# Summing a block's last two bunches in one step, and moving the stores and the reads of its rows, in a two-layer graph network kernel

## The chip, the cores and the metric

One core of a Trainium2 chip runs the whole kernel. The time is the device time of one execution in microseconds (us). Three runs of the kernel before the change took 3989.87, 3995.48 and 4023.41 us; the median is 3995.48.

Five engines take part: PE (matrix products; PEld is its loading of weights), DVE (vector operations), ACT (functions and copies), POOL (here it only issues the gathers) and SP (here it only issues transfers). Each has its own queue of instructions, carries them out in order, and waits for the others by semaphores.

## What is computed

A graph has 12500 nodes with 128 features and 200000 edges, sorted by their destination. An edge's relation is one of ten, the argmax of ten of its 42 attributes. A layer takes the mean of the source rows over the edges of each (destination, relation), multiplies it by that relation's matrix, sums over the relations, and adds the node's own row times a root matrix and a bias:

```python
def _rgcn_layer(x, src, dst, edge_type, w_rel, root, bias):
    seg = dst * NUM_REL + edge_type
    xs = x[src]
    sums = segment_sum(xs, seg, N * NUM_REL)
    cnt = segment_sum(ones, seg, N * NUM_REL)
    mean = (sums / maximum(cnt, 1.0)[:, None]).reshape(N, NUM_REL, -1)
    return einsum('nrd,rdo->no', mean, w_rel) + x @ root + bias
h = relu(_rgcn_layer(x, ..., w_rel1, root1, b1))
out = layernorm(x + _rgcn_layer(h, ..., w_rel2, root2, b2))
```

## The kernel before, in words

**Tiles and bunches.** The edges lie in 1563 tiles of 128 (`NT`), in the order of their destination. Four tiles make a bunch (`QB`, line 31), so layer 1 has 391 bunches and walks them in steps `p` (loop at line 948). A tile's work is this. POOL gathers the 128 source rows from DRAM by an indirect transfer into a tile `g` (`gathered`, line 751). DVE builds a mask `oh` that holds, for each edge, a one in the column of its relation and its destination within a window of twelve nodes (`ones`, line 765), and ACT scales it by one over the count (`weighted`, line 757). PE multiplies the gathered rows by the mask into a PSUM tile `zp` (line 983). DVE adds that into `cc`, a ring in SBUF that holds the sums of 1024 nodes for ten relations (`sum_into`, line 797). The window's place in the ring is a register that DVE loads.

**Two layers at once.** The ring has two halves, one for each layer. A node's hidden row `h` is final when all edges into it have been added; since edges are sorted, nodes become final in order, in blocks (`starts`: 46 of 256 nodes, then six of 128 or less). Once a block is final its hidden rows are stored into a table `XH`, beside the input rows. Later tiles gather from that table rows of 256 features, input and hidden, and PE multiplies both parts, so that an edge whose source is already known is done for both layers in one gather. An edge whose source isn't known yet finds zeros there. What was missed is done in layer 2: the first `T0` tiles, gathered before the table was of use, are gathered again from the full hidden table `hD`, and the missed edges of the later tiles are regrouped on the chip into new tiles and gathered from `hD` too (lines 1461 to 1537).

**Two tables and epochs.** There are two copies of `XH`, because a copy can't be written while gathers read it. Epochs are counted in rows of 11 tiles (`RT`). From epoch k on (`first_seen[k]`, line 125) gathers read the copy that holds the rows of all blocks up to k; the next epoch reads the other copy (`table_of`, line 127). A block's rows go into the copy of its own epoch first (`stored(hb, first, k)`, line 875), and into the other copy once that epoch has begun (line 879). Which tile first reads a block is fixed ahead by a rule: `finished_in(k)` (line 109) is the step that finishes block k, and the epoch begins `READY` bunches (six, line 54) behind that step, rounded up to a whole row of 11 tiles. The same rule fixes `T0` (166 tiles) and the size of what layer 2 regroups.

**The order of the work around a block's end.** The order on each engine is the order in which the program is written (a manual schedule, line 1042). A step p issues the gathers of bunch p, the products of bunch p on PE (`products`, line 976), then side jobs, then the sums of bunch p - 2 (`BEHIND`, line 37; `sums`, line 986). Where the bunch just summed is the last that a block needs, `finish(k, t)` (line 844) follows in the same step: PE projects the block by ten matrices and the root (`projected`, line 732, lines 739 and 742). The rest is put off to later steps by a list of due times, in units u of one bunch: `rows_out` after one step (ACT adds the bias and cuts off below zero, line 672; PE turns the rows, line 864), `rows_kept` after two (ACT copies them, line 871; SP stores them into `hD` and the table), the clearing of the ring's places (line 722), the second layer's projection (`second`) after three, the load and the turning of the next block's input rows.

**Buffers.** `g` has seven buffers (`GB`); once the table is read a bunch takes one of them, so the gather of bunch p needs the products of bunch p - 7 done. `zp` has five PSUM tiles, two a bunch. `oh` has seven. The turned and projected blocks (`pf`) share two PSUM tiles.

The lines that matter most:

```python
q = p - BEHIND                                            # 988
while done < NBLK and t0 + n >= done_after(done):         # 1002
    finish(done, t)
...
assert k <= K0 or now + QB >= first_seen[k - 1]           # 877
...
todo.at(t + (1 if k == NBLK - 2 else 2) * u, rows_kept)   # 892
```

Of the kernel before, what the change touches and what calls it, by code (L numbers as in the profile page):

```python
# [30 lines left out]
QB = 4  # L31
# [5 lines left out]
BEHIND = 2  # L37
# [13 lines left out]
SPLIT = 63  # L51
LEAD = 40
LAST = 40
READY = 6
LOW = 1 << 13
TOPN = (1 << 14) - 1
OFF = 80
# [7 lines left out]
def rgcn_resnorm_kernel(ctx: ExitStack, tc: tile.TileContext, x, src, dst, attr, w_rel1, root1, b1,  # L65
# [26 lines left out]
    def done_after(k):  # L92

        if k == NBLK - 1:
            return NT
        f = starts[k + 1] / N
        t = int((E * f + 5 * (E * f * (1 - f)) ** 0.5) / P) + 2
        if t >= NT:
            return NT
        return min(a + n for a, n in parts if a + n >= t)  # L100
# [7 lines left out]

    def finished_in(k):

        return -(-done_after(k) // QB) - 1 + BEHIND

    K0, K1 = KSEEN
    NR = (NT - QB * (finished_in(K0) + READY)) // RT
# [722 lines left out]
    def layer_1():  # L837

        todo = Later()
        done = 0  # L840
# [3 lines left out]
        def finish(k, t):  # L844

            if k < NBLK - 2:
                todo.run(END)
            if k not in fTs:
                xbs[k] = rows_in(k)
                fTs[k] = features_in(k, 0, xbs[k])  # L850
            u = QB if t < NT else 0
            folded(ALL, k, WN)
            po = [projected(k, 0, (rsb[0], fTs[k]))]
            both = starts[k + 1] > bounds(T0)[0] if k + 1 < NBLK else True
            reused = starts[k] + RN < N
            assert not reused or t + 7 * u <= (starts[k] + RN - OFF - WN) // STEP

            def rows_out(_):
                a = po.pop()
                a = fin_a.setdefault(k, shifted(a, k, 0))  # L860
                pr = ps_f.tile([P, 4, C], F32, name="pf")
                n0, n, subs = block(k)
                for i, h in subs:
                    nc.tensor.transpose(pr[:h, i, :], a[:, i * P:i * P + h], ident)
                po.append(pr)

            def rows_kept(now):
                pr = po.pop()
                hb = fin.tile([P, 2, C], F32, name=f"hb{k % 2}")
                for p, s in spans(k):  # L870
                    nc.scalar.activation(hb[:p, s], pr[:p, s], AF.Copy)
                rows_dma(hb, hD, k, True)
                if k <= K1:
                    first = 0 if k <= K0 else (k - K0) % 2
                    stored(hb, first, k)
                    if k < K1:
                        assert k <= K0 or now + QB >= first_seen[k - 1]
                        when = t + 8 * QB if k < K0 else first_seen[k] + 2 * QB
                        todo_late.append((when, lambda t: stored(hb, 1 - first, k)))

            def second(_):
                po.append(projected(k, 1, (rsb[1], fin_a.pop(k)), more=both))

            def second_kept(_):
                n0, n, _ = block(k)
                p2 = po.pop()
                t2 = fin.tile([P, 3 * P], F32, name="v")
                nc.scalar.activation(t2[:, :n], p2[:, :n], AF.Identity, bias=bsb[1])
                nc.sync.dma_start(T2[:, n0:n0 + n], t2[:, :n])

            todo.at(t + u, rows_out)
            todo.at(t + (1 if k == NBLK - 2 else 2) * u, rows_kept)
            if reused:
                todo.at(t + 2 * u, lambda t: cleared(0, k, 0))
                todo.at(t + 3 * u, lambda t: cleared(0, k, 1))
            if k < NBLK - 1:
                todo.at(t + (9 if k >= NBLK - 3 else 3) * u, second)
                todo.at(t + (9 if k >= NBLK - 3 else 4) * u, second_kept)
            else:
                todo.run(t)  # L900
                todo.run(END)
                todo.at(t, second)
                todo.at(t, second_kept)
            if both:
                w = 10 if k >= NBLK - 3 else 5
                todo.at(t + w * u, lambda t: cleared(1, k, 0))
                todo.at(t + (w + 1) * u, lambda t: cleared(1, k, 1))
            if k + 1 < NBLK - 1:
                def fetch(t):
                    xbs[k + 1] = rows_in(k + 1)  # L910

                def turn(t):
                    n0, n, subs = block(k + 1)
                    pt = ps_f.tile([P, YB], F32, name="pf")
                    for i, h in subs:
                        nc.tensor.transpose(pt[:, i * P:i * P + h], xbs[k + 1][:h, i, :], ident[:h, :h])
                    po.append(pt)

                def turned_kept(t):
                    n0, n, subs = block(k + 1)  # L920
                    pt = po.pop()
                    fTs[k + 1] = fin.tile([P, 3 * P], F32, name="fT")
                    nc.scalar.activation(fTs[k + 1][:, :n], pt[:, :n], AF.Copy)  # L923
                todo.at(t + u, fetch)
                w = 2 if k == NBLK - 3 else 4
                todo.at(t + w * u, turn)
                todo.at(t + (w + 1) * u, turned_kept)
# [20 lines left out]
        for p in range(-AHEAD, NPT + BEHIND):  # L948
            if p + AHEAD < NPT:
                t0, n = parts[p + AHEAD]  # L950
                ohs[p + AHEAD] = ones(keyE[:, t0:t0 + n], iotaP, n, WN)
            if 0 <= p + AHEAD - 1 < NPT:
                t0, n = parts[p + AHEAD - 1]
                for j in reversed(range(n)):
                    weighted(ohs[p + AHEAD - 1], j, KW, wE[:, t0 + j:t0 + j + 1])
            if p < 0:
                continue
            t = p * QB
            if p < NPT:
                t0, n = parts[p]  # L960
                plain = t0 + n <= T0
                if not plain or p % 2 == 0:
                    g = gpool.tile([P, GQ * C], F32, name="g")
                slot = [p % 2 * QB + j if plain else 2 * j for j in range(n)]
                for j in range(n):
                    i = t0 + j
                    idx = idxE[:, i:i + 1]
                    if i < T0:
                        gathered(g, slot[j], x, idx, 1)
                    else:  # L970
                        gathered(g, slot[j], XH[table_of(i)], idx, 2)
                made = (g, ohs.pop(p), slot)
            if p == NPT - CP // 4:
                xbs[NBLK - 1] = rows_in(NBLK - 1)
                fTs[NBLK - 1] = features_in(NBLK - 1, 0, xbs[NBLK - 1])
            def products(g, oh, slot):
                t0, n = parts[p]
                zps[p] = [ps_z.tile([P, YB], F32, name="zp") for _ in range(0, n, 2)]
                for j in range(n):
                    i = t0 + j  # L980
                    zp, a = zps[p][j // 2], j % 2 * 2 * KW
                    for l in (0, 1) if i >= T0 else (0,):
                        nc.tensor.matmul(zp[:, a + l * KW:a + (l + 1) * KW], g[:, (slot[j] + l) * C:(slot[j] + l + 1) * C],  # L983
                                         oh[:, j * KW:(j + 1) * KW], start=True, stop=True)

            def sums():
                nonlocal done, offs, row
                q = p - BEHIND
                if q < 0:
                    return  # L990
                t0, n = parts[q]
                if t0 % CT == 0:
                    row = rows_.tile([1, CT], I32, name="row")
                    nc.scalar.dma_start(row, b_i[t0 // CT:t0 // CT + 1, :])
                if t0 % G == 0:
                    m = min(G, NT - t0)
                    offs = offsets(row[:, t0 % CT:t0 % CT + m], t0, m, bounds)
                for j in range(n):
                    i = t0 + j
                    sum_into(ALL if i >= T0 else ONE, zps[q][j // 2], j % 2 * 2 * KW, offs[i % G], WN)  # L1000
                del zps[q]
                while done < NBLK and t0 + n >= done_after(done):
                    finish(done, t)
                    done += 1

            if p < NPT - 1:
                products(*made)
            jobs.run(t)
            sums()
            if p == NPT - 1:  # L1010
                products(*made)
            made = None
            todo.run(t)
            for d in [d for d in todo_late if d[0] <= t]:
                todo_late.remove(d)
                d[1](t)
# [692 lines left out]
```

## Time and profile before

| what | value |
|---|---|
| median of three runs | 3995.48 us (3989.87 to 4023.41) |
| the profiled execution | 4014.34 us |
| its span, first to last instruction | 4012.5 us |
| mean granted PE clock, share of full | 0.759 |
| gathers of x alone, of the table, of `hD` in layer 2 | 166; 1397; 166 + 695 |
| layer 1, by POOL's gathers | up to about 2557 us |
| bytes read from DRAM, written | 322.86 MB, 57.89 MB |

How to read it: the page gives for each engine its busy time, for groups of instructions their line, operation, tiles, count, busy time and mean, and then the idle time that the engine had before them and what ended it. "issue" is idle time that nothing in the profile ended, "remote" an end that the profile can't name. The view of waits adds up such idle times by engine and line: total us, times, longest. The timeline has one row for an instruction or a run of like ones: start, duration, engine, line, operation, count, and in brackets the idle time ahead of it with its releaser. The view of stretches has for each stretch of time the busy time and the count (x) of each engine, of all its instructions or of one line's.

### The profile page before, as it was taken

To read this page: it belongs to the slowest core of one execution; us is meant where nothing else is said; L and a number is where in the kernel's file an instruction comes from. 1 tells how busy PE (TensorE), PEld (TensorE's weight loads), DVE (VectorE), ACT (ScalarE), POOL (GpSimd) and SP (SyncE) were. 2 spreads that over 40 slices of the span, in tenths; PEclk is the share of its full clock that TensorE was granted. 3 is DMA by queue.
4 is the path that set the end of the run, shared out by engine and by line. 5 is a ranking of instruction groups with operands and counts; after the bars stand their busy time and mean duration, and the time that the engine had idled before them with its cause. 6 is when DMAs were issued, how large, how long until landed. Compare 5 with 4: busy or idle time off the path is not lost.

```text
span 4012.5 us, 42414 instructions
## 1 busy us (share of the span) xinstructions
PE 2486.8 (62%) x11883; PEld 2056.9 (51%) x11883; DVE 2033.2 (51%) x5464; ACT 1303.6 (32%) x3179; POOL 2294.7 (57%) x2436
## 2 busy tenths in 40 slices
PE   1555676666665666666676767624546766766666
PEld 0444565555555565555565656614444444545455
DVE  4453454555444546453444344339465555655565
ACT  2341233222332233233332323313324344444443
POOL 6645555565555565655565666466455656665661
PEclk7666777877777777777777877856768887877888
DMA  4562433343333333333333333311112122222121
GB/s 133 176 201 87 125 99 118 96 127 98 121 92 115 104 112 105 112 109 110 109 114 102 98 102 95 89 45 53 42 45 58 54 58 62 59 61 60 56 62 33
DMA packets 265374, 370.96 MB, mean 92 GB/s; under 512 B 51280, under 2 KB 197365, under 8 KB 265134
## 3 DMA queue, kind: packets, MB, share of 16 engines
q0 software_dynamic: 99920, 250.57, 21.4%
q1 hardware_dynamic: 111587, 91.97, 7.4%
q10 hardware_dynamic: 53627, 25.62, 2.2%
q8 instruction: 102, 1.67, 0.2%
q14 instruction: 138, 1.13, 0.1%
HBM read 322.86 MB, written 57.89 MB: 95 GB/s over the span
## 4 chain that ended last, share of the span: by engine, by line
PE 39%; issue 24%; another core or an unknown queue 14%; DVE 14%; ACT 2%; POOL 2%; DVEq 1%; DMA 1%; SPq 0%; ACTq 0%; POOLq 0%
PE zp L983 18%; PE pf L739 13%; DVE cc L797 5%; PE zp L1502 2%; POOL g L751 2%; DVE oh L775 2%; PE zq L1502 1%; PE pf L742 1%; ACT oh L757 1%; DVEq L782 1%; DVE oh L765 1%; DVE cc L1162 1%; PE pf L559 1%; PE pf L557 1%
## 5 line engine op out<-in xcount | busy, mean ns | idle before, releaser
L751 POOL DMA_INDIRECT g<-XH,idxE x1397 | 1321.3, 946 | 981.4 <-issue 444.6
L983 PE MATMUL zp<-oh,g 128*128 128x120 f32 x5920 | 1027.6, 327 | 727.0 <-issue 636.2
L797 DVE TENSOR_TENSOR cc<-cc,zp 128x240 f32 (+11 forms) x2193 | 841.3, 384 | 1150.6 <-remote 662.7
L983 PEld LDWEIGHTS zp<-oh,g 128*128 128x128 f32 x5920 | 943.4, 239 | 813.7 <-issue 731.8
L751 POOL DMA_INDIRECT g<-hD,idxB x695 | 657.1, 945 | 450.5 <-issue 180.6
L739 PE MATMUL pf<-cc,w 128*128 128x256 f32 (+3 forms) x3020 | 767.1, 412 | 174.9 <-issue 82.9
L739 PEld LDWEIGHTS pf<-cc,w 128*128 128x128 f32 x3020 | 616.8, 216 | 305.8 <-issue 113.5
L757 ACT ACTIVATE oh<-oh,wE 128x120 f32<-128x120 f32 x1729 | 531.2, 382 | 352.8 <-DVE oh L765 255.9
L757 ACT ACTIVATE oh<-oh,wB 128x150 f32<-128x150 f32 (+23 forms) x771 | 338.7, 482 | 442.1 <-DVE oh L775 236.4
L1502 PE MATMUL zp<-oh,g 128*128 128x120 f32 (+20 forms) x1260 | 346.8, 418 | 210.2 <-issue 79.8
L1502 PEld LDWEIGHTS zp<-oh,g 128*128 128x128 f32 x1260 | 238.4, 239 | 288.1 <-issue 212.4
L722 ACT ACTIVATE cc<-zero 128x1280 f32<-128x1280 f32 (+3 forms) x274 | 336.6, 1231 | 74.8 <-DVE cc L797 58.2
L775 DVE TENSOR_TENSOR oh<-wide,keyB 128x480 f32<-128x480 f32 (+17 forms) x400 | 230.3, 576 | 177.7 <-remote 100.3
L672 ACT ACTIVATE a<-pf,b 128x256 f32<-128x256 f32 (+1 forms) x50 | 23.2, 465 | 734.5 <-remote 313.8
L765 DVE TENSOR_TENSOR oh<-bank,keyE 128x480 f32<-128x480 f32 x391 | 253.5, 649 | 0.0
L1502 PE MATMUL zq<-oh,g 128*128 128x160 f32 (+21 forms) x614 | 183.3, 433 | 97.4 <-issue 54.9
L751 POOL DMA_INDIRECT g<-hD,idxE x166 | 157.9, 951 | 104.8 <-issue 44.5
L751 POOL DMA_INDIRECT g<-in_x_dram,idxE x166 | 156.8, 945 | 96.2 <-issue 46.9
L1502 PEld LDWEIGHTS zq<-oh,g 128*128 128x128 f32 x614 | 119.7, 229 | 147.3 <-issue 124.1
L797 DVE TENSOR_TENSOR cc<-cc,zq 128x160 f32 (+21 forms) x307 | 120.0, 391 | 61.2 <-issue 14.3
L923 ACT ACTIVATE fT<-pf 128x256 f32<-128x256 f32 (+1 forms) x50 | 18.5, 370 | 401.8 <-remote 344.6
L548 DVE TENSOR_TENSOR eqb<-bank,kh 128x1344 bf16<-128x1344 f32 (+2 forms) x65 | 100.7, 1551 | 25.4 <-remote 19.0
(241 smaller groups left out, 1288.7 us busy)
## 6 DMA issues: line engine op xcount, KB each, us to landing
m<-in_edge_attr_dram SPq DMA_DIRECT2D x48, 672.0 KB
g<-XH,idxE POOLq DMA_INDIRECT x1397
XH<-in_x_dram ACTq DMA_DIRECT2D x24, 512.0 KB
XH<-zero ACTq DMA_DIRECT2D x24, 512.0 KB
XH<-hb SPq DMA_DIRECT2D x87, 128.0 KB
g<-hD,idxB POOLq DMA_INDIRECT x695
xb<-in_x_dram SPq DMA_DIRECT2D x72, 128.0 KB
hD<-hb SPq DMA_DIRECT2D x46, 128.0 KB
```

Source lines behind the costliest of these rows:

```text
L548: nc.vector.tensor_tensor(eq[:p], kpP[:p, None, :R].to_broadcast([p, DB, R]), fore, op=ALU.is_equal)
L557: nc.tensor.matmul(pc[:p], identb[:p, :p], eq[:p, k:k + 4, L:], start=(d + k == 1), stop=False)
L559: nc.tensor.matmul(pc[:p], identb[:p, :p], back, start=False, stop=(d + k + 3 == L))
L722: nc.scalar.activation(cc[:, l, h * H:(h + 1) * H, o:o + n], zero[:, None, :n].to_broadcast([P, H, n]), AF.Copy)
L739: nc.tensor.matmul(po[:, :n], wsb[l][:, r, :], cc[:, l if ring is None else ring, r, o:o + n], start=(r == 0), stop=False)
L751: nc.gpsimd.indirect_dma_start(out=g[:, j * C:(j + n) * C], out_offset=None, in_=table, in_offset=bass.IndirectOffsetOnAxis(ap=idx, axis=0))
L757: nc.scalar.activation(s, s, AF.Copy, scale=w)
L765: nc.vector.tensor_tensor(o.rearrange("p (t m) -> p t m", m=m), cols[:, None, :m].to_broadcast([P, n, m]), keys[:, :, None].to_broadcast([ ...
L775: nc.vector.tensor_tensor(to, a, b, op=ALU.is_equal)
L797: nc.vector.tensor_tensor(s, s, z, op=ALU.add)
L983: nc.tensor.matmul(zp[:, a + l * KW:a + (l + 1) * KW], g[:, (slot[j] + l) * C:(slot[j] + l + 1) * C], oh[:, j * KW:(j + 1) * KW], start=Tr ...
L1502: nc.tensor.matmul(zp[:, j * m:(j + 1) * m], gt[:, b * C:(b + 1) * C], oh[:, j * m:(j + 1) * m], start=True, stop=True)
```

## The change

Three things are changed. A step whose last products complete a block (up to block 43) sums two bunches, p - 2 and p - 1, so that the block is finished one step sooner; the step after it then has nothing to sum. The copy and the stores of the block's rows (`rows_kept`) come one step after the finish, in the step of `rows_out`, instead of two. And `READY` is eight and is counted from the new, earlier step. Since the rows can now be ready before the copy that they go into is free, a store that would come too early is put on the list of later stores, due in the last bunch before the older epoch ends. With the new rule `T0` is 177 instead of 166, layer 2 regroups into 687 tiles instead of 695, and an epoch begins where it did or one row of 11 tiles later.

```diff
-READY = 6
+READY = 8
...
     def finished_in(k):
-        return -(-done_after(k) // QB) - 1 + BEHIND
+        return -(-done_after(k) // QB)
...
                     first = 0 if k <= K0 else (k - K0) % 2
-                    stored(hb, first, k)
+                    free = first_seen[k - 1] - QB if k > K0 else 0
+                    if now >= free:
+                        stored(hb, first, k)
+                    else:
+                        todo_late.append((free, lambda t: stored(hb, first, k)))
                     if k < K1:
-                        assert k <= K0 or now + QB >= first_seen[k - 1]
...
-            todo.at(t + (1 if k == NBLK - 2 else 2) * u, rows_kept)
+            todo.at(t + u, rows_kept)
...
             def sums():
+                last = p - BEHIND
+                if done <= K1 and 0 < p <= NPT and sum(parts[p - 1]) >= done_after(done):
+                    last = p - 1
+                for q in [q for q in sorted(zps) if q <= last]:
+                    summed(q)
+
+            def summed(q):
                 nonlocal done, offs, row
-                q = p - BEHIND
-                if q < 0:
-                    return
                 t0, n = parts[q]
```

## The prediction

> **What bounds the kernel now.** I read the page first (busy shares, queues, groups), then the waits, then the timelines of POOL and PE side by side in layer 1, then the stretches. No engine is full: POOL has 2295 us of 4012, PE 2487.
>
> ```profile
> PE 2486.8 (62%) x11883; PEld 2056.9 (51%) x11883; DVE 2033.2 (51%) x5464; ACT 1303.6 (32%) x3179; POOL 2294.7 (57%) x2436
> ...
> q8 instruction: 102, 1.67, 0.2%
> ...
> L751 POOL DMA_INDIRECT g<-XH,idxE x1397 | 1321.3, 946 | 981.4 <-issue 444.6
> ```
>
> So engines wait for each other. PE, POOL and their neighbours tell whom. From the list of all waits, the two that concern this change most (total us, times, longest):
>
> ```profile
> PEld zp L983 <- issue: 731.8, 526, 24.2
> ...
> POOL g L751 <- DMA XH<-hb: 183.5, 27, 16.1
> ```
>
> The last row is what the edit is about: the gather waits, 27 times, until a block's stored rows have landed in the table. Does anybody wait for the gather in turn? The view of line 751 lists who waited for it:
>
> ```profile
>   PE zp L983: 28.2, 21
> ```
>
> 28 us in the whole program. The gathered rows lie ready long before PE takes them, so the 183.5 us aren't 183.5 us of path. Layer 1 is paced by PE, and PE's largest loss is "issue", time in which it waited for nothing that the profile shows. The two timelines around such a loss, POOL first, then PE (start, us, operation, idle before it):
>
> ```profile
> 1019.11 0.95 POOL L751 DMA_INDIRECT g<-XH,idxE  x1 [0.30 <-issue]
> 1030.19 0.94 POOL L751 DMA_INDIRECT g<-XH,idxE  x1 [10.13 <-DMA XH<-hb]
> 1031.43 0.95 POOL L751 DMA_INDIRECT g<-XH,idxE  x1 [0.30 <-issue]
> ...
> 1057.67 0.94 POOL L751 DMA_INDIRECT g<-XH,idxE  x1 [0.30 <-issue]
> 1063.03 0.94 POOL L751 DMA_INDIRECT g<-XH,idxE  x1 [4.41 <-PE zp L983]
> ```
>
> ```profile
> 1035.85 3.28 PE L983 MATMUL zp<-oh,g 128*128 128x120 f32 x28
> 1039.45 0.26 PE L983 MATMUL zp<-oh,g 128*128 128x120 f32 x1 [0.32 <-issue]
> 1040.85 0.26 PE L983 MATMUL zp<-oh,g 128*128 128x120 f32 x1 [1.14 <-issue]
> ...
> 1061.99 0.36 PE L983 MATMUL zp<-oh,g 128*128 128x120 f32 x1 [1.04 <-issue]
> 1062.71 4.69 PE L983 MATMUL zp<-oh,g 128*128 128x120 f32 x24 [0.36 <-issue]
> 1067.24 4.49 PE L739 MATMUL pf<-cc,w 128*128 128x256 f32 x20
> ```
>
> After the store's wait POOL runs 23 gathers without a break, 1030 to 1059, one each 1.25 us. PE runs at full speed (28 matmuls in 3.3 us) for nine microseconds of this, then issues one matmul every 1.4 to 2.8 us, and is itself again at 1062.7, when POOL has paused. The reader is to see that the cost of a store's wait isn't the wait: it is the long run that follows it.
>
> How long the run is depends on how far ahead of its first reader a block's rows are stored. Worked out from the code, first reader less store step is 4 to 4.75 bunches for blocks 16 to 19, 5 to 5.75 for 20 to 23, 6 to 6.5 for 24 to 26, and the same sawtooth again for 27 to 37, since a block has 32 tiles and an epoch of the table 33. Cutting layer 1 at these borders and counting line 983's matmuls (128 for 32 tiles) gives an experiment that the trace holds already:
>
> ```profile
> core 0: us, PE busy (x) PEld busy (x), PEclk, DMA share, GB/s
> 972.00:1188.00 216.00, 84.04 (x495) 76.70 (x494) 0.76 0.36 108
> 1188.00:1403.00 215.00, 89.49 (x531) 82.16 (x530) 0.77 0.36 107
> 1403.00:1551.00 148.00, 61.95 (x389) 56.91 (x388) 0.79 0.37 114
> 1551.00:1762.00 211.00, 85.97 (x490) 77.95 (x488) 0.75 0.36 109
> 1762.00:1968.00 206.00, 86.84 (x508) 78.12 (x506) 0.77 0.36 110
> 1968.00:2110.00 142.00, 64.86 (x384) 60.35 (x384) 0.79 0.37 109
> 2110.00:2279.00 169.00, 64.49 (x371) 59.67 (x372) 0.75 0.34 99
> 2279.00:2430.00 151.00, 67.34 (x390) 61.70 (x390) 0.77 0.35 101
> ```
>
> Rows 1 and 4 (gap 4 to 4.75): 427 us for 985 matmuls, 55.5 us per 128. Rows 2 and 5 (gap 5 to 5.75): 421 for 1039, 51.9. Rows 3, 6 and 8 (gap 6 and 5.75 to 6.25): 441 for 1163, 48.5. Row 7 begins with a gap of 4 again: 58.3. All eight: 1458 for 3558, 52.45. Same code, same work, and the pace improves with the gap.
>
> **The change, part by part.**
>
> Store and read. The finish of a block k up to 43 comes one bunch sooner, and the rows' copy and stores come in the step after it instead of the second: the store is two bunches sooner. The reader moves by one bunch in the rule, and rounding to rows of 11 tiles leaves most epochs where they were and puts some 2.75 bunches back. The gap becomes 7 to 9.5. The gather of bunch p also needs the buffer that bunch p-7 has used (seven of them), so a gap of 7 or more means that the buffer, not the store, ends POOL's wait: the store's waits go, and what is late next is PE releasing the buffer. Seven stores (blocks 4, 5, 19, 20, 30, 31, 39) are deferred by one bunch, as their table is still read; their gap is 6 or more. Gain: bounded by none (pace stays 52.45) and by the pace of the large gaps (48.5). I take 49.7, seven tenths of the way: the large-gap stretches are near the buffer's limit already, so they show the new regime best, but they were cut where they look best and three like stretches differ by 2 us (47.3 to 49.6). 313 bunches of layer 1, 39 blocks, read tables after stores: 39 x (52.45 - 49.7) = 107 us.
>
> A Trainium skill rule speaks against this. "Runtime: NRT & Kernel Launch", section "Instruction fetch mechanics", says that instructions come in 16 KiB blocks by the sequencer's own DMA queue and that crossing a block is mostly hidden. The page of the profile agrees on the blocks (q8: 102 packets, 1.67 MB, 16 KB each), but PE's slow stretches of 20 us would then need another cause, one that POOL's breaks need not mend; by the rule the gain is 0 and the sum below is +43 instead of -64.
>
> Two bunches in one step. In the old order PE does the products of bunch q+2 and then projects the block, which needs the sums of bunch q. In the new order it projects after the products of q+1. Rows from a block's end (DVE):
>
> ```profile
> 1855.16 1.72 DVE L797 TENSOR_TENSOR cc<-cc,zp 128x240 f32 x4
> ...
> 1856.79 0.65 DVE L765 TENSOR_TENSOR oh<-bank,keyE 128x480 f32<-128x480 f32 x1
> ```
>
> The four adds are 1.72 us. The second half of the products of q+2 waits for the first two of them anyway (five PSUM tiles, two a bunch), so what is new is the other half, 0.9 us, and DVE has nothing to add in the step after. Lower bound 0 (DVE ahead), upper bound all adds and a mask, 2.4 us. I take 0.9, as DVE's adds do follow close on PE: 44 blocks x 0.9 = +40 us (0 to 106). The projection itself (20 matmuls, 4.49 us) only moves, as do the load and turning of the next block's x and the second layer's projection; the ACT clears move with them.
>
> ACT now copies the rows right after the shift in the same step, and stands between them for PE's two transposes; behind it waits the scaling of the next bunch's masks, which PE needs a bunch later. ACT is a third busy, so 0 (0 to 0.4 us, the length of a transpose or copy, a block; 18 us in all). If the cover went, PE would wait those 18.
>
> SP. The three stores of a block go out earlier, ahead of the loads queued behind them (x, attributes); SP's order is otherwise the same. From SP's own waits:
>
> ```profile
> SPq L634 <- ACT hb L871: 956.3, 45, 51.8
> ```
>
> SP stands waiting for the copied rows 45 times, so what is queued behind them gains and nothing loses. Each store must wait for the gathers that still read its table; these were issued some bunches ahead, so 0.
>
> Later tables. There are 177 first tiles instead of 166 and 687 regrouped instead of 695 in layer 2. The two stretches of layer 2:
>
> ```profile
> 2577.00:2844.00 267.00, 105.97 (x494) 91.43 (x495) 155.33 (x294) 58.80 (x175) 157.92 (x166) 0.62 0.20 56
> 2844.00:3930.00 1086.00, 708.83 (x2609) 518.83 (x2607) 613.47 (x1772) 447.93 (x943) 657.07 (x695) 0.79 0.20 57
> ```
>
> 11 x 267/166 = +17.7, 8 x 1086/695 = -12.5; in layer 1 eleven tiles lose half of their matmuls, 22 x 0.1 = -2. Net +3 (-12 to +18). POOL's first wait for the table is filled with eleven x gathers, but PE isn't waiting there: 0.
>
> Sum: -107 + 40 + 3 = -64 us. The profiled execution took 4014.3 (span 4012.5) and would take 3950; it lies 19 us above the median of the three runs, 3995.5, which I predict from: 3931, say 3930.
>
> **The rivals.**
>
> Hidden anyway. PE's slow issue hangs on where it stands in its program, not on POOL's breaks; POOL stops at the buffer instead of the store and nothing follows. For: PE waited 28 us for gathers in all. Against: 55.5, 51.9 and 48.5 at the same code. Pace 52.45, plus 0 to 43 for the tighter sum: 3996 to 4038, middle 4015.
>
> Slower: longer runs. POOL's breaks are what lets PE recover (1062.7 above). Without the store's wait POOL may run 20 gathers and more each time, and the pace is that of the smallest gaps, 55.5: 39 x 3.05 = +119, +43: about 4157. For: slow issue begins some nine microseconds into a run. Against: with all seven buffers full POOL must stop for PE, and such stops come sooner the slower PE is. It decides when runs of over 20 gathers become more frequent than one a block.
>
> The store still ends the wait. The deferred ones, or a store that lands late, keep the row "DMA XH<-hb" alive; then the pace moves only half: 39 x 1.4 = -55, +43: 3985.
>
> **How the numbers follow.** Forecast 0.50, hidden 0.27, longer runs 0.20, store still late 0.03. The forecast's own range: pace 48.5 and no cost for the sum (-154 + 3: 3845) to pace 50.7 and 1.5 us a block (-68 + 66 + 3: 3997). The range 3850 to 4060 holds nearly all of the forecast, of "hidden" and of "still late", and a quarter of "longer runs". About 1% (40 us) is what a measurement of this kernel can tell from no change. Faster by more (under 3955) is most of the forecast, 0.45; within 1% the rest of it and the two middle rivals, 0.33; slower 0.22.
>
> **What would show it.** Right: the waits no longer have "DMA XH<-hb" with more than some 20 us, POOL's waits are for PE; the eight stretches show one pace near 50 us per 128 matmuls, with no 55; "PEld zp L983 <- issue" falls by about 100. The tighter sum shows as waits of PE's line 739 on DVE, up by 40. Wrong: pace at 52 with POOL at the buffer (hidden), or PE's "issue" grown and POOL runs of 20 and more (longer runs). The step I trust least is that the gap's effect on the pace goes on to a gap that no stretch of this trace has.

## The result, and the profile after

The changed kernel took 3986.60 us (median of 16 runs, 3977.58 to 4007.79), the kernel before 4004.07 beside it (16 runs): 0.996 times the time before, with a 95% interval of 0.9944 to 0.9975. Run again at another time, on another chip: 0.9966 (0.9952 to 0.998). So it is faster by some 12 to 17 us, where 64 were forecast. The profiled execution has a span of 3977.4 us.

The list of waits of the changed kernel (total us, times, longest). Its products are line 986, where the kernel before had 983:

```profile
PEld zp L986 <- issue: 445.5, 335, 24.3
...
PEld pf L739 <- issue: 160.7, 114, 9.8
POOL g L751 <- DMA XH<-hb: 159.3, 27, 12.5
...
PEld pf L739 <- DVE cc L797: 114.0, 38, 10.1
...
PEld pf L739 <- DVE cc L729: 74.6, 12, 16.8
```

The last two rows in the kernel before:

```profile
PEld pf L739 <- DVE cc L797: 61.1, 22, 10.6
...
PEld pf L739 <- DVE cc L729: 10.9, 6, 2.5
```

Two of the forecast's signs came true: the issue wait of the products fell by 286 us, where some 100 were forecast, and line 739 waits 53 us more for DVE's sums (114.0 against 61.1). It waits another 64 us more for line 729, which folds the ring's end into its start ahead of a block's projection. But the row that was to vanish is there, 159.3 us in 27 waits where it was 183.5 in 27. And the issue that went isn't in the time. The view of lines between 400 and 2400 us, for the kernel before and then for the changed one (count, busy and mean, then the idle time ahead, with what ended it):

```profile
L983 PE MATMUL zp<-oh,g 128*128 128x120 f32 x4933 | 844.8, 324 | 584.3 <-issue 533.6 <-DMA g<-XH,idxE 16.8 <-remote 15.8
L739 PE MATMUL pf<-cc,w 128*128 128x256 f32 x1540 | 384.9, 404 | 31.1 <-issue 28.9 <-DVE cc L797 1.1
```

```profile
L986 PE MATMUL zp<-oh,g 128*128 128x120 f32 x4899 | 796.2, 319 | 400.3 <-issue 320.3 <-ACT oh L757 46.7 <-remote 17.5
L739 PE MATMUL pf<-cc,w 128*128 128x256 f32 x1523 | 420.5, 428 | 214.7 <-issue 108.1 <-DVE cc L797 65.3 <-DVE cc L729 39.0
```

584.3 + 31.1 = 615.4 us idle ahead of the two groups before, 400.3 + 214.7 = 615.0 after. PE did as much in the same 2000 us (4933 and 4899 matmuls); its idle time only moved from one line to the other.

The eight stretches of the forecast in the changed kernel, line 986 alone:

```profile
972.00:1188.00 216.00, 87.40 (x579) 82.04 (x578) 0.79 0.37 108
1188.00:1403.00 215.00, 80.42 (x486) 74.85 (x487) 0.75 0.36 107
1403.00:1551.00 148.00, 63.12 (x373) 60.09 (x371) 0.75 0.38 115
1551.00:1762.00 211.00, 84.38 (x544) 80.43 (x544) 0.80 0.36 106
1762.00:1968.00 206.00, 82.69 (x452) 75.31 (x453) 0.74 0.37 110
1968.00:2110.00 142.00, 58.62 (x374) 54.32 (x373) 0.82 0.36 104
2110.00:2279.00 169.00, 62.87 (x421) 59.80 (x421) 0.82 0.36 107
2279.00:2430.00 151.00, 61.10 (x358) 56.24 (x357) 0.74 0.35 102
```

1458 us for 3587 matmuls is 52.0 us per 128, against 52.45, and the stretches still differ: 47.8 in the first, 58.3 in the fifth. So the pace of layer 1 hardly moved. Comparing the two traces bunch by bunch, the last products of bunch 50 end 24 us sooner (360.6 against 384.2), and those of bunch 363 20 us sooner (2398.0 against 2418.2). In these two executions the gain lies at the start and behind bunch 363, not in the 313 bunches that the forecast counted.

Why is the store still waited for? SP's and POOL's timelines around one switch of tables, where gather 661 is the first to read block 18:

```profile
1061.35 0.36 SPq L634 DMA_DIRECT2D hD<-hb  x1
1062.11 0.26 SPq L634 DMA_DIRECT2D XH<-hb  x1
...
1073.46 0.38 SPq L892 DMA_DIRECT2D T<-v  x1
1073.89 0.43 SPq L634 DMA_DIRECT2D XH<-hb  x1
```

```profile
1071.83 0.94 POOL L751 DMA_INDIRECT g<-XH,idxE  x1 [2.01 <-PE pf L742]
1079.03 0.95 POOL L751 DMA_INDIRECT g<-XH,idxE  x1 [6.25 <-DMA XH<-hb]
```

There are two stores into the table, 12 us apart. The first is block 18's own, which the change moved. The second is block 17's second copy. It goes into the same table, and the code makes it due two bunches into epoch 17, so 6.25 bunches ahead of this reader. POOL's wait ends behind the second store, not the first. Counting SP's stores against the order in the code for epochs 5 to 43, the later of the two was block k-1's second copy in all 39 in the changed kernel, and in 24 of 39 already in the kernel before (in 18 of these both go out in the same step). Its gap to the reader is 5.5 to 6.25 bunches, and 3 to 3.25 where two epochs lie two rows of tiles apart (blocks 5, 20, 31, 39). The first copies did move, to 6 to 9.25 bunches, much as forecast.

For the experiments I use one number from each trace: the sum of POOL's pauses ahead of the first gather of these 39 epochs. It is 278 us before and 250 after.

### The profile page after: what moved, and what is told of

Its sections match the earlier page's. It is cut to its first block, busy times and chain, and to the rows that moved or that the text cites. A ratio compares the mean times of both kernels' runs of the same rounds, so it can differ in the third digit from the quotient of the medians.

```text
span 3977.4 us, 42318 instructions
## 1 busy us (share of the span) xinstructions
PE 2461.4 (62%) x11844; PEld 2030.3 (51%) x11844; DVE 2031.5 (51%) x5459; ACT 1299.2 (33%) x3180; POOL 2299.2 (58%) x2439
## 5 line engine op out<-in xcount | busy, mean ns | idle before, releaser
L986 PE MATMUL zp<-oh,g 128*128 128x120 f32 x5898 | 959.9, 320 | 520.9 <-issue 394.3
L986 PEld LDWEIGHTS zp<-oh,g 128*128 128x128 f32 x5898 | 896.7, 232 | 591.9 <-issue 445.5
L739 PE MATMUL pf<-cc,w 128*128 128x256 f32 (+4 forms) x3000 | 794.4, 423 | 346.0 <-issue 130.5
L757 ACT ACTIVATE oh<-oh,wB 128x150 f32<-128x150 f32 (+22 forms) x762 | 333.7, 482 | 415.7 <-DVE oh L775 200.8
L1509 PEld LDWEIGHTS zp<-oh,g 128*128 128x128 f32 x1276 | 238.6, 237 | 314.2 <-issue 260.4
L722 ACT ACTIVATE cc<-zero 128x1280 f32<-128x1280 f32 (+1 forms) x274 | 336.1, 1229 | 104.8 <-DVE cc L797 84.8
L751 POOL DMA_INDIRECT g<-hD,idxE x177 | 168.7, 953 | 121.8 <-issue 47.2
L1509 PE MATMUL zq<-oh,g 128*128 128x160 f32 (+23 forms) x602 | 188.5, 450 | 70.9 <-issue 31.8
L751 POOL DMA_INDIRECT g<-in_x_dram,idxE x177 | 167.4, 946 | 101.0 <-issue 49.0
L797 DVE TENSOR_TENSOR cc<-cc,zq 128x160 f32 (+23 forms) x301 | 119.9, 398 | 50.4 <-issue 14.5
L891 ACT ACTIVATE v<-pf,b 128x256 f32<-128x256 f32 (+2 forms) x52 | 23.9, 460 | 221.2 <-PE pf L742 106.0
```

What stands on the lines that cost most here:

```text
L722: nc.scalar.activation(cc[:, l, h * H:(h + 1) * H, o:o + n], zero[:, None, :n].to_broadcast([P, H, n]), AF.Copy)
L739: nc.tensor.matmul(po[:, :n], wsb[l][:, r, :], cc[:, l if ring is None else ring, r, o:o + n], start=(r == 0), stop=False)
L751: nc.gpsimd.indirect_dma_start(out=g[:, j * C:(j + n) * C], out_offset=None, in_=table, in_offset=bass.IndirectOffsetOnAxis(ap=idx, axis=0))
L757: nc.scalar.activation(s, s, AF.Copy, scale=w)
L797: nc.vector.tensor_tensor(s, s, z, op=ALU.add)
L1509: nc.tensor.matmul(zp[:, j * m:(j + 1) * m], gt[:, b * C:(b + 1) * C], oh[:, j * m:(j + 1) * m], start=True, stop=True)
```

## The experiments

The kernel before took 3968 to 4004 us on some chips (all profiles so far are from one), called the slow kind below, and 3074 to 3076 on three others, the fast kind. Whether this belongs to the chip itself or to its condition then isn't shown. Ratios are to the kernel before on the same chip.

**Which part does what.** Four kernels on one chip of the slow kind. The early sum undone:

```diff
-READY = 8
+READY = 7
-        return -(-done_after(k) // QB)
+        return -(-done_after(k) // QB) - 1 + BEHIND
...
-                if done <= K1 and 0 < p <= NPT and sum(parts[p - 1]) >= done_after(done):
-                    last = p - 1
```

> The changed kernel with the early sum undone: a block's last two bunches are summed in two steps again and the block is finished one bunch later; the copy and the stores still come one step after the finish, and tables and reads stay where the change put them (READY 7 counted from the later step, T0 177). Theory A (traded): between 400 and 2400 us PE's idle for issue fell by 147 us with the change, as the forecast wanted, and new waits of about 175 us stand in its place (line 739 for DVE +103, products for the mask's scaling +46, transposes for ACT +26); without the early sum most of these go and the time is 100 to 150 us under the changed kernel, 3840 to 3890. Theory B (forecast's price): the early sum costs 40 us, so 3945. Theory C (exchanged): PE's idle only changes its name, because the round of POOL's buffers, PE and DVE sets the pace; within 15 us of the changed kernel, 3970 to 4000.

Measured: 1.0084 (1.0054 to 1.0113), 4035 us. All three theories missed. Theory A had read the new waits of line 739 as a price that would come back; it falls. The pauses ahead of the epochs grew to 291 us.

With the copy two steps after the finish as well, so that only the later read is left:

> The kernel before with only the later read (READY 7, T0 177, deferred stores where a table is still read): no early sum, and the copy two steps after the finish as before. The forecast's gap theory: the gap of the first copies is 5 to 7.5 bunches instead of 4 to 6.5, so the pace improves by about one stretch of the quoted table (3 us per 128 matmuls), 39 x 3 = 117 us less, 3890. Exchange: only the start is shorter, where the first reads of the table wait for its zeros (some 9 to 20 us), 3985 to 3995.

Measured: 0.9967 (0.9949 to 0.9985), 3990 us; pauses 254 us. That is the whole change's gain (0.996) from one number, READY. As in the changed kernel, it lies at the start: bunch 50 ends 26 us sooner, and the 313 bunches behind it take 2037 us, against 2034 in the kernel before. So the later read alone gives as much as the whole change, though by the due times the first copies' gap grew by only 0.6 bunches on the mean instead of 2.5.

The second copy sooner, in the changed kernel:

```diff
-                        when = t + 8 * QB if k < K0 else first_seen[k] + 2 * QB
+                        when = t + 8 * QB if k < K0 else first_seen[k] - QB
```

> The changed kernel with one number changed: a block's second copy is stored three bunches sooner (in the step that ends the older epoch, instead of two bunches into the new one). In the changed kernel's trace the last store ahead of each first gather of an epoch is that second copy. If it is what keeps the row of POOL's waits for the store alive (159.3 us, 27 times), the row falls under 30 us. Forecast's gap theory: with the store's wait gone the pace term is paid in full, 50 us less than the changed kernel, 3935. Exchange: the buffer ends POOL's waits instead and the time stays, 3975 to 3995.

Measured: 0.9631 (0.9608 to 0.9654), 3858 us, 128 less than the changed kernel on its chip, where the gap theory had expected 50; pauses 83 us. POOL's wait and the products of PE in the same 2000 us:

```profile
POOL g L751 <- DMA XH<-hb: 43.6, 9, 9.6
```

```profile
L986 PE MATMUL zp<-oh,g 128*128 128x120 f32 x5233 | 857.5, 322 | 362.6 <-issue 290.9 <-ACT oh L757 47.4 <-remote 11.2
```

PE does 5233 matmuls where the changed kernel did 4899 and the kernel before 4933: 2000 x 128 / 5233 = 48.9 us per 128, against 51.9 in the kernel before. The step from one to the other is 3.0 us, where the forecast had 2.75. The 313 bunches take 1905 us instead of 2037 and 2034. The row of waits fell to 43.6 and not under 30: of the 12 epochs with a pause over 2.5 us left, eight have a first copy as the last store, 7 to 7.75 bunches ahead, and four (blocks 5, 20, 31, 39) have both copies in one step, 6 bunches ahead.

> Both: late sum, and second copy three bunches sooner. Traded plus gap theory: the sum of the two gains, 3790 to 3850. Traded alone: as the run with the late sum, 3840 to 3890, whatever the second copy does. Exchange: 3970 to 4000, with POOL's waits for the store gone.

Measured: 0.9816 (0.979 to 0.9842), 3927 us; pauses 171, wait 93.0. It lies between the theories. Here the first copies are about a bunch nearer than in copy2_early (7.0 against 7.9 on the mean), so the sum and the gap are mixed.

**The early sum by itself.** With the late sum, READY 8 gives the first copies about the gap that copy2_early has. The first two attempts met chips of the fast kind.

> The same epochs as in the run with READY 9, second copy sooner, but without the early sum (finish one bunch later, so the first copies have the gap that the run copy2_early had, less deferred ones). It tells whether the early sum itself is worth or costs anything. Theory D: only the gap counts, so 3850 to 3870, like copy2_early (3858), wait about 40 us. Forecast's price: 40 us less than copy2_early for the sum, 3820. Rival G (the early sum is itself a gain of some 60 us, because the step after it has nothing to sum): 3910 to 3930.

Fast kind: 1.0042 (1.0029 to 1.0056).

> Once more, since the last four ran on a chip where the kernel before takes 3076 us and PE's slow issue does not occur (runs of slow issue 6 us in all, against some 660 us on the chip of 4002 us); there the edits cost or gave nothing but the later table (13 us). If the chip is of the slow kind: it tells whether the early sum is worth anything by itself. Only the gap counts: 3850 to 3870, like copy2_early (3858), wait about 40 us. Forecast's price for the sum: 3820. Early sum a gain of its own of some 60 us: 3910 to 3930. On a chip of the fast kind: 3076 + 12.

Fast kind: 1.0047 (1.0033 to 1.0061).

> As before under this name: on a chip of the slow kind only the gap counts: 3850 to 3870, like copy2_early (3858), store wait about 40 us; forecast's price for the sum: 3820; early sum a gain of its own of some 60 us: 3910 to 3930. On a chip of the fast kind 3076 + 13.

Slow kind: 0.9654 (0.9635 to 0.9672), wait 39.5, pauses 66. Of the kernel before's 4002 us that would be 3863, as expected if only the gap counts, and not the 3820 of the forecast's price. Beside copy2_early's 0.9631 (0.9608 to 0.9654), on another chip of that kind, the early sum is worth nothing that can be told at nearly the same gap (8.1 against 7.9 bunches on the mean). The 69 us by which late_sum_copy2 was slower come with a nearer store. The 48 us of late_sum aren't explained by it: the store due last is the same second copy as in the changed kernel, 5.6 bunches ahead on the mean in both. They stay open.

**READY 9, and the copy two steps after the finish.** Both met a chip of the fast kind.

> Changed kernel, second copy three bunches sooner, and READY 9: half of the epochs begin a row of 11 tiles (2.75 bunches) later, T0 stays 177. Theory D: what is left of the store's wait (43.6 us, 9 times) is at the first copies with the smallest gaps; it falls under 20 us and the time by about as much, 3830 to 3850. Rival F (the gain is used up when the buffer takes over): wait gone, time 3850 to 3865.

Measured: 1.0045 (1.0031 to 1.0058), 3089.6 us.

> As READY 9 with the second copy sooner, but the rows are copied and stored two steps after the finish, as in the kernel before; the gap of the first copies is that of copy2_early. In copy2_early PE's transposes waited 77.6 us for ACT between 400 and 2400 us and the products 47.4 us for the mask's scaling; in the kernel before 11.3 and 0.6. If the copy right behind the shift is what makes ACT late, these rows go back and the time is 30 to 60 us under copy2_early, 3800 to 3830. If they are exchanged for other waits: 3850 to 3865.

Measured: 1.0047 (1.0033 to 1.0061), 3089.7 us. So on this kind neither the early sum (1.0042 without it, same epochs) nor the copy's place makes a difference that can be told. What these three share is the later table, and their 13 us lie where it would cost: the products of bunch 363 end at 1827 to 1828 us as in before_copy2 below, and from there to the end they take 1260 to 1263 us against 1244. No run has the later table alone. On the slow kind these two weren't run.

**The second copy alone**, in the kernel before:

> The kernel before with the second copy alone stored three bunches sooner. In the runs so far the time goes with POOL's wait for stores (row DMA XH<-hb): 216.6 us at 4035, 183.5 at 4002, 180.2 at 3990, 159.3 at 3987, 93.0 at 3927, 43.6 at 3858. Theory D (both copies bind): in the kernel before the first copies are the nearer ones, 4 to 6.5 bunches ahead of their reader against 6.25 of the second, so moving the second alone changes little: wait 150 to 185, time 3975 to 4005. Rival E: the second copy alone was what mattered, as SP's and the transfers' order goes by it; then about 128 us go as they did in the changed kernel, 3875.

Fast kind: 1.0003 (0.9994 to 1.0012).

> The kernel before with the second copy alone three bunches sooner, once more. On a chip of the slow kind: both copies bind, so little changes: wait 150 to 185 us, 3975 to 4005; rival, the second copy alone was what mattered: 3875. On a chip of the fast kind: 3076, no change.

Fast kind: 1.0001 (0.9992 to 1.001).

> The kernel before with the second copy alone three bunches sooner, on the slow kind of chip if it comes: both copies bind, wait 150 to 185 us, within 0.7% of the kernel before; rival, the second copy alone was what mattered, 3% less.

Slow kind: 0.9947 (0.9926 to 0.9967), pauses 233, and a wait lower than expected:

```profile
POOL g L751 <- DMA XH<-hb: 118.1, 19, 14.0
```

So neither copy pays much alone: the first sooner with a later read 0.4%, the second sooner 0.5%, both 3.7%.

The rows of before_copy2 on the fast kind show why the stores don't matter there (waits of POOL, then its gathers from the table):

```profile
POOL g L751 <- issue: 654.8, 2149, 0.3
POOL g L751 <- PE zp L983: 27.7, 91, 0.3
```

```profile
L751 POOL DMA_INDIRECT g<-XH,idxE x1397 | 1321.7, 946 | 425.6 <-issue 379.6 <-PE zp L983 26.5 <-DMA g<-XH,idxE 10.4
...
L983 PEld LDWEIGHTS zp<-oh,g 128*128 128x128 f32 x5920 | 880.9, 225 | 481.9 <-issue 192.0 <-DMA g<-XH,idxE 146.2 <-PE zp L983 86.9
```

POOL issues one gather each 1.25 us (946 ns and 0.30) and its longest wait of these two kinds is 0.3 us; it bounds the program: 2424 gathers x 1.25 = 3030 of 3073 us. PE's weight loads wait 192.0 us for issue, against 731.8. POOL runs through its gathers from the table without a break, and PE isn't slow.

**The changed kernel again:**

> The changed kernel itself once more, on whichever kind of chip it meets. Slow kind (kernel before near 4002): 3987 again, slow issue of PE some 460 us in the trace against 660. Fast kind (kernel before near 3076, no slow issue, POOL never waits for stores): POOL is the bound there, the change adds 11 gathers in the tiles gathered twice and saves 8 in layer 2, 3 x 1.25 = 4 us, and the stretch of layer 2 pays 11 x 1.6 less 8 x 1.5, so 3076 + 4 to 6; if the early sum or the copy cost anything of its own it would show here: 40 us by the forecast's price, 3120.

Slow kind: 0.9966 (0.9952 to 0.998), 3956 us against 3968; wait 157.0, pauses 253.

**The wait or what follows it.** Fewer buffers for the gathers, so that POOL is stopped by PE before it comes to a store:

```diff
-GB = 7
+GB = 5
```

> The kernel before with five gather buffers instead of seven, nothing else: gather p needs products p - 5, so POOL mostly stops at the buffer before it comes to a store that isn't there yet. Theory R (the forecast's: a store's wait costs through the long run after it): POOL's runs get shorter, PE's slow issue falls well under the 663 us of the kernel before, and the time falls to 3850 to 3930 on the slow kind of chip, though POOL has less lead. Theory W (the wait itself is the path, or POOL's lead is what carries PE): the store's wait turns into waits for the buffer and the time is the kernel before's or more, 4000 to 4080. On the fast kind of chip POOL never waits, so either 3076, or more if five buffers are too few.

Measured, slow kind: 0.9509 (0.9494 to 0.9524), 3772 us. No store is moved, and the time falls by 5%, more than either theory had. POOL's waits in this kernel:

```profile
POOL g L751 <- issue: 665.4, 2138, 4.6
...
POOL g L751 <- remote: 259.3, 109, 8.6
POOL g L751 <- PE zp L983: 134.9, 60, 13.9
...
POOL g L751 <- DMA XH<-hb: 31.0, 7, 8.7
```

The store's wait fell from 183.5 to 31.0, and the waits for PE's products rose by 10 us only (125.1 before). Theory W, that it would turn into waits for the buffer, falls. If a pause over 1.5 us ends a run, POOL's runs are little shorter on the mean, 10.5 gathers against 11.2, but 354 of the 1397 gathers lie in runs of 14 and more, where it was 648. Between the runs lie pauses of some 2 us, as here:

```profile
1043.83 0.95 POOL L751 DMA_INDIRECT g<-XH,idxE  x1 [0.30 <-issue]
1046.82 0.94 POOL L751 DMA_INDIRECT g<-XH,idxE  x1 [2.05 <-PE zp L983]
...
1061.01 0.95 POOL L751 DMA_INDIRECT g<-XH,idxE  x1 [0.30 <-issue]
1064.32 0.94 POOL L751 DMA_INDIRECT g<-XH,idxE  x1 [2.36 <-remote]
```

> The changed kernel with the second copy three bunches sooner and five buffers. The store's wait is gone already (43.6 us with seven). Theory R: runs of at most one or two bunches, slow issue under the 236 us of copy2_early, time 3800 to 3850 where the kernel before takes 4002. Lead theory: two bunches less lead cost, 3870 to 3950.

Measured, slow kind: 0.9449 (0.9428 to 0.947), 3752 us, the fastest of all; the store's wait is gone from the list, pauses 22. Once more, beside four buffers:

> The fastest version so far, again beside the two with four buffers: 0.945 on the slow kind of chip; on the fast kind the later table's cost, 1.002 to 1.005, and more if five buffers are too few there.

Fast kind: 1.0046 (1.0032 to 1.006), as expected for the later table. But POOL's gathers are already 10 us later at bunch 20 than in before_copy2 (114 against 104 us, on another chip), long ahead of any use of the table, so most of the 14 us doesn't come from the later table.

> The kernel before with four buffers. With five it took 0.951 of its time on the slow kind of chip (slow issue 331 us instead of 663). Theory R goes on to four: slow issue under 250 us, ratio 0.93 to 0.95. Where the lead becomes too short (PE waits for gathers: 28 us with seven), it turns back: 0.96 to 1.0. On the fast kind, where POOL bounds and never waits, fewer buffers can only cost: 1.00 to 1.05.

Fast kind: 1.0105 (1.009 to 1.0121).

> The changed kernel with the second copy sooner and four buffers; with five 0.945. Theory R: 0.92 to 0.945; lead too short: over 0.95. Fast kind: 1.00 to 1.05.

Fast kind: 1.0096 (1.008 to 1.0111). Four buffers cost 1% there. What they do on the slow kind wasn't measured.

All kernels on the slow kind. "Slow issue" is the time in which PE issued five or more instructions in a row 0.45 to 3 us apart, counted in the trace. The count depends on its bounds: from start to start of matmuls it is 690 us in the kernel before, 504 in the changed one, 285 in copy2_early, 373 in before_gb5, and 85 in before_copy2 on the fast kind.

| kernel | pauses ahead of 39 epochs | wait row XH<-hb | slow issue | ratio |
|---|---|---|---|---|
| late_sum | 291 | 216.6 | 661 | 1.0084 |
| before | 278 | 183.5 | 663 | 1 |
| later_read | 254 | 180.2 | 670 | 0.9967 |
| after_again | 253 | 157.0 | 506 | 0.9966 |
| changed kernel | 250 | 159.3 | 462 | 0.996 |
| before_copy2_c | 233 | 118.1 | 662 | 0.9947 |
| late_sum_copy2 | 171 | 93.0 | 475 | 0.9816 |
| copy2_early | 83 | 43.6 | 236 | 0.9631 |
| late_sum_copy2_ready8_c | 66 | 39.5 | 285 | 0.9654 |
| before_gb5 | 57 | 31.0 | 331 | 0.9509 |
| copy2_gb5 | 22 | none | 156 | 0.9449 |

From before to copy2_early the pauses fall by 195 us and the time by 3.69% of 4002 = 148. Where the pauses nearly stay (the changed kernel), slow issue fell by 200 us and the time by 16.

The place of the last store, taken from the traces as PE's bunches between its issue and its first reader's, orders most of these times: on the mean 4.5 in the kernel before, 4.7 in before_copy2_c and in later_read, 5.1 in the changed kernel, 5.4 in late_sum_copy2, 6.2 in copy2_early, 6.4 in late_sum_copy2_ready8_c. Two kernels fall out of the order: late_sum (4.8, and slower) and before_gb5 (4.2, and much faster).

## Why the prediction was wrong, step by step

**"The gap becomes 7 to 9.5 ... the store's waits go."** This is the step that failed. I counted one store into a table for each block; there are two, and the second copy of the block before stayed at 3 to 6.25 bunches. So the row "DMA XH<-hb" stayed at 159.3 us in 27 waits; with the second copy sooner too it fell to 43.6. The second copy's line stands right below the edited ones in the code, with its due time. The sign was in the trace too: in the kernel before, the second copy already went out last ahead of 24 of 39 epochs, in six of them in a later step. The table of stretches sorted the pace by the gap of the first copies. In the kernel before they were due last in 15 epochs and in one step with the second copy in 18, so the dependence was real, but it couldn't be carried past the gap of the second copies.

**The pace term, -107.** On the changed kernel it is near 0: 52.0 us per 128 against 52.45, with products from bunch 50 to 363 in 2037 us against 2034. With the second copy out of the way it comes: 48.9 against 51.9, 39 x 3.0 = 117 us, and the 313 bunches take 132 us less than in the changed kernel (1905 against 2037). So the gap's effect on the pace, and its size, were right, and the edit didn't reach it. That it works through the long run behind the wait is borne out only in part: in the kernel before, the products' idle time for issue is 0.05 us per gather while POOL is in the first three of a run, 0.39 at the eighth to eleventh and 0.96 at the twelfth to fifteenth (in before_gb5 0.02, 0.42 and 0.59). This goes together; that the run is the cause isn't shown.

**"The buffer, not the store, ends POOL's wait" from a gap of 7.** Not quite. In copy2_early the first copies have 6 to 9.25 bunches and POOL still pauses over 2.5 us at 12 epochs, eight of them with a gap of 7 and more. By the trace a first copy is issued 1.6 bunches of PE's work behind the start of its step there, on the mean, and must land; at these 12 epochs 2.7 to 5.4 us pass from the last store's issue to the gather's start.

**Two bunches in one step, +40.** The wait appeared (+53 us on line 739 for the sums, +64 for line 729), but it cost nothing that can be told: the late sum at nearly the same gap gives 0.9654 against 0.9631, and on the fast kind, at the same epochs, 1.0042 against 1.0045. A wait that appears on PE isn't a price while PE's other idle time gives way by as much, as the 615 us before and after show.

**ACT's copy right behind the shift, 0.** Right on the fast kind (1.0047 and 1.0045). On the slow kind it is open: late_sum and later_read differ by this copy's place, and by 1.2% in time, with 291 and 254 us of pauses. I have no cause for it.

**SP, 0.** "What is queued behind them gains" was too easy: the second copy stands in that queue behind the next block's rows and `T`, and nothing made it sooner.

**Later tables, +3.** Too high for this kind of chip. later_read has 3990 against 4002. POOL's wait for the table's zeros is 37.6 us before and 28.7 after, and I had put this at 0, since PE didn't wait there; from bunch 51 on POOL's gathers run 8 to 21 us ahead of those before, and PE's products of bunch 50 end 24 us sooner (26 in later_read). In layer 2 of the changed kernel:

```profile
2556.00:2830.00 274.00, 111.04 (x509) 95.14 (x510) 158.91 (x309) 61.49 (x181) 169.61 (x178) 0.62 0.21 57
2830.00:3900.00 1070.00, 703.99 (x2601) 514.09 (x2599) 611.00 (x1770) 444.09 (x943) 649.03 (x686) 0.80 0.21 58
```

The first stretch is 274 us against 267, the second 1070 against 1086: -9 where I had +17.7 - 12.5 = +5. On the fast kind, where POOL bounds, the three kernels with 11 tiles more and 4 fewer take 13 us more, 7 x 1.25 = 9 of it for the gathers.

**The blocks of instructions.** The instruction queue moved 102 packets of 16 KB on both kinds of chip, with a median of 0.98 us a packet in the kernel before on the slow kind and 1.02 in before_copy2 on the fast kind, while slow issue was 663 us on the one and 6 on the other. Of the 690 us of slow issue in the kernel before (start to start), packets of the instruction queues were in transit for 17 us. So the trace speaks against these packets as its cause; what goes on ahead of a packet the profile doesn't show. The Trainium skill, "Runtime: NRT & Kernel Launch", section "Instruction fetch mechanics", says that crossing a block of instructions is mostly hidden. As far as packets in transit go, the trace of the kernel before agrees. By that rule the forecast's sum was +43 instead of -64; the measured time is near neither.

**The rivals.** The nearest in time was "the store still ends the wait" (3985, given 3 in 100), but for another reason than the two it named: not deferred or late first copies, but a store it hadn't counted. "Hidden anyway", that slow issue hangs on PE's place in its program, is refuted by copy2_early, by five buffers and by the fast kind. "Longer runs" came only a little: runs of over 20 gathers were 10 where the kernel before had 6, far from one a block.

What stays open: why PE issues slowly on one kind of chip, and whether the length of POOL's runs by itself brings it there. Five buffers make long runs rarer and remove most of the store's waits at once, so they don't separate the two; they do show that the wait's own microseconds needn't be paid elsewhere. On the fast kind POOL runs without a break and PE isn't slow, so a long run alone isn't enough.

## What to carry to other kernels

Before crediting an edit with a wait, list every transfer that the wait depends on, with its due time; the edit helps only if it moves the one that comes last, and the next one is often close behind. A wait that appears in the trace isn't yet a cost, nor one that goes a gain: add up the idle time ahead of all of an engine's groups, before and after. Fewer buffers can be faster than more: with five instead of seven this kernel took 0.951 of its time on one kind of chip, and with the second copy sooner 0.945 there and 1.005 on the other.

## What the runs showed that I had not expected

Chips of two kinds ran the same program at 3968 to 4004 us and at 3074 to 3076. A gather (946 ns) and a product's matmul (324 and 319 ns in the middle of the program) take as long on both; what differs is idle time: PE's weight loads of line 983 wait 731.8 us for issue on one and 192.0 on the other. The granted PE clock is 0.759 in the kernel before on the slow kind and 0.834 in before_copy2 on the fast. Edits that win 3.5% and 5.5% on the one (late_sum_copy2_ready8, copy2_gb5) cost 0.4% to 0.5% on the other, so a result belongs to the kind of chip that gave it.
